# Inner values, outputs and divisions of a fused decoder layer set in other steps

## The chip, the cores and the metric

One core of one Trainium2 chip runs the whole kernel. The metric is device time in microseconds (us). Five engines take part: TensorE (PE in the profile; its weight loads are PEld), VectorE (DVE), ScalarE (ACT), GpSimd (POOL) and SyncE (SP), which here only issues transfers. Each engine works through its own list of instructions, and semaphores between them keep the data right.

## The reference

A decoder layer over `x` of 4 batches x 1024 tokens x 512 features, all float32, with a context of 4 x 1024 x 384. Cut to what matters:

```python
x = x + gated_attention(layernorm(x))             # 16 heads of 32; an aperture and an expression gate; a rotation of the result
q = layernorm(x) @ Wq + bq; k = ctx @ Wk + bk; v = ctx @ Wv + bv
x = x + softmax(q k^T / sqrt(32)) v @ Wo + bo     # cross attention, 16 heads
s = layernorm(x) @ Win + bin                      # 64 units
h = relu(s[..., None] * W1 + b1)                  # each with 16 inner values
g = sum_h(h * W2) + b2
x = x + g @ Wout + bout
```

The last four lines are 64 tiny networks of one input, 16 inner values and one output each, between two matrix products.

## The kernel before, in words

The work is cut into eight units: units 0 to 3 are the gated attention of batches 0 to 3, units 4 to 7 the cross attention of the same batches. A unit has two halves of 512 query tokens, and a half has 4 groups of 4 heads (`g`) with 8 key tiles of 128 (`kt`): 32 steps. The text names a step unit/half/step, so 5/1/4 is the fifth step of the second half of unit 5. The order of every engine's instructions is the order in which the program writes them; nothing reorders them.

A step (`step` in `attention`) does this, in this order:

- `issue_due(False)` runs what an earlier step left for this one (divisions).
- `scores`: TensorE computes two score tiles `s` of 128 x 1024 (L574), ScalarE makes the exponentials `e` of each (L579), VectorE adds them into `es` (L585, L587), two additions a step in units 4 to 6 and none at `kt` 0. There are two `s` tiles and six `e` tiles.
- `issue_due(True)` runs what was left to stand behind these additions.
- `late.pop(0)()` is the previous step's `times`: the exponentials times the values, into `av` (L601).

Eight steps end a group. ScalarE copies `av` out (L618), one step later the sums go through L631 and L632, and `sum_d` carries them through memory into another layout; two steps later `divide` takes reciprocals (L668), which travel through `rec_d` and come back spread over all partitions as `recb` (L671, L675); two steps after that `multiply` (L681) writes the divided values over the queries. `after(steps, f, behind)` puts such a part off: with `behind` it runs in `issue_due(True)`, without it in `issue_due(False)`.

Between the steps `run` lays other work, the filler. `beside(u, hf)` lists it: projections for the next unit, the output projection and layer norm of the half before (`post`: "wo", "load", "o", "ln"), and in units 5 to 7 the small networks of earlier halves. Every item has a load, about its matmuls in units of four; `run` spreads the sum of the loads evenly over the 32 steps. An item without a load goes into the step where the item before it ended. `pause(n)` makes n items that carry a load of 1 and do nothing. `weave(a, b)` sets the items of `a` evenly among those of `b`.

The small networks of a half go through these items: "s" makes `s` (L841), 17 items "h" make the inner values on ScalarE (`hid`, L858, two buffers) and add each, one item later, into `g` on VectorE (L862, L864). Two items "out" then multiply with `Wout`; each takes two tiles of the pool `f` (L875), adds them to the residual (L881) and sends it out (L883). The pool `f`, from `bank()`, has two PSUM tiles of 128 x 512 and serves every projection too (L87, evacuated at L280 to L284, L525, L770). `held` keeps a half whose inner values are not all made. The first few are made at the end of one `beside`, the rest at the start of the next by `end(items)`, which weaves them into `items` and sets the outputs behind. The last unit has no next projections and uses pauses.

Of the kernel before, what the change touches and what calls it, by code (L numbers as in the profile page):

```python
# [63 lines left out]
def moderate_path(tc: tile.TileContext, a: dict, out: bass.AP, flag: bass.AP):  # L64
    nc = tc.nc
    x = a["x"]
    with ExitStack() as st:
# [130 lines left out]
        def rotate(c):  # L198
            def f():
                pw = bank()  # L200
                columns(pw, rot[:, c, :], raw[0][:, c, :], start=True, stop=True)
                nc.vector.tensor_copy(raw[0][:, c, :], pw)
                if c == NC - 1:
                    nc.sync.dma_start(wout_d, raw[0])
            return [(1, f)]
# [130 lines left out]
        order = [(ph, b) for ph in range(2) for b in range(B)]  # L336
        n = len(order)
# [4 lines left out]
        def after(steps, f, behind=False):  # L342

            soon.append((tick[0] + steps, behind, f))
# [206 lines left out]
        def attention(u, hf):  # L551
# [8 lines left out]
            def apart(g):  # L560
                return 2 if u + 1 < len(order) else 3
# [90 lines left out]
            def divide(g, i, both, c):  # L652
                if shared:
                    both_ = p2.tile([P, sums, INNER], F32, tag="c2", name="both_")
                    nc.vector.tensor_tensor(both_, c[:, 0:sums, 0, :], c[:, 0:sums, 1, :], ALU.add)
                else:
                    both_ = c[:, 0:1, 0, :]
                if ph == 0:

                    den = p2.tile([P, INNER], F32, tag="den", name="den")  # L660
                    nc.vector.scalar_tensor_tensor(
                        den, both_[:, 0, :], 1e-8, me["iap", hf][:, g, :], ALU.mult, ALU.mult
                    )
                    nc.vector.tensor_tensor(den, den, both_[:, 1, :], ALU.add)
                else:
                    den = both_[:, 0, :]
                rec = p2.tile([P, INNER], F32, tag="rec", name="rec")
                nc.vector.reciprocal(rec, den)  # L668
                nc.vector.tensor_reduce(marks[:, i : i + 1], den, AX.X, ALU.add)
                nc.vector.tensor_reduce(marks[:, NS + i : NS + i + 1], rec, AX.X, ALU.add)  # L670
                nc.sync.dma_start(rec_d[i % 4].rearrange("j (q e) -> (j q) e", e=INNER), rec)  # L671

                all_ = p1.tile([P, HALF], F32, tag="recb", name="recb")
                for j in range(HG):
                    nc.sync.dma_start(  # L675
                        all_[j * DH : (j + 1) * DH, :], rec_d[i % 4][j : j + 1, :].to_broadcast([DH, HALF])
                    )
                after(apart(g), lambda: multiply(g, both, all_))

            def multiply(g, both, all_):  # L680
                nc.vector.tensor_tensor(me["q", hf][:, g, :], both[:, 0, :], all_, ALU.mult)  # L681
                me["divided", hf] = g
# [235 lines left out]
        def weave(light, items):  # L918

            first, second = sum(light, []), sum(items, [])  # L920
            out, done = [], 0
            for n, f in enumerate(first):
                upto = (2 * n + 1) * len(second) // (2 * len(first))
                out += second[done:upto] + [f]
                done = upto
            return [out + second[done:]]
# [14 lines left out]
        def pause(load):  # L941
            return [[(1, None)] * load]

        n = len(order)
        pres = [pre(u) for u in range(n)]

        def one(f):
            return [[(0, f)]]

        ending = []  # L950
        held = []

        def ahead(u, what):

            return one(lambda: pres[u]["load"](what))

        def some(half, k):

            h, half["h"] = half["h"][:k], half["h"][k:]
            return h  # L960

        def beside(u, hf):

            last = post(u, 0) if hf else post(u - 1, 1) if u else None
            end = lambda items: weave(held[0]["h"], items) + held.pop()["out"] if held else items
            if u + 1 == n:
                h, out = held[0]["h"], last["wo"] + last["load"]
                k = min(len(h), 6)
                if hf:
                    ending.append(post(u, 1))  # L970
                    out += ending[0]["wo"]
                out += weave(h[0:k], pause(12)) + weave(h[k:], last["o"]) + held.pop()["out"]
                out += (ending[0]["load"] if hf else []) + weave(last["ln"], pause(5)) + last["xT"]
                out += weave(last["b"], pause(8))
                out += weave(last["tr"], pause(3)) + last["s"] + weave(some(last, 8), pause(14))
                held.append(last)
                return out
            p = pres[u + 1]
            x, ln, xT, tr, k, q, v = (p[i] for i in ("x", "ln", "xT", "tr", "k", "q", "v"))
            next_ = pres[u + 2] if u + 2 < B else None  # L980
            if u + 1 < B:
                if hf == 0:
                    if last:
                        out = x[1] + last["wo"] + last["load"] + ahead(u + 1, "v") + k[0][0:1] + p["g"][0] + k[0][1:] + p["gt"][0]
                        out += weave(ln[1], last["o"]) + xT[1] + weave(last["ln"], v[0][0:2])
                    else:
                        out = one(fold_bv) + x[1] + k[0][0:1] + [rotate(c) for c in range(NC)]
                        out += ahead(u + 1, "v") + p["g"][0] + k[0][1:2] + [[(4, fold_bv)]] + weave(ln[1], k[0][2:])
                        out += p["gt"][0] + v[0][0:1] + xT[1] + v[0][1:2]
                    return out + tr[1] + v[0][2:3] + p["g"][1] + v[0][3:] + p["gt"][1]  # L990
                if not next_:
                    out = k[1] + ahead(u + 1, "q") + last["wo"] + last["load"] + v[1] + ahead(u + 2, "k") + last["o"]
                    return out + weave(last["ln"], q[0][0:2]) + q[0][2:] + pres[u + 2]["ctx"][0] + q[1]
                out = next_["x"][0] + k[1][0:2] + last["wo"] + last["load"] + weave(next_["ln"][0], k[1][2:] + v[1])
                out += ahead(u + 1, "q") + ahead(u + 2, "k") + last["o"]
                out += weave(last["ln"], q[0][0:2]) + q[0][2:] + next_["xT"][0] + q[1][0:3] + next_["tr"][0] + q[1][3:]
                if u == 1:
                    out = one(lambda: load_networks(0)) + out + one(lambda: load_networks(1)) + one(fold_bin)
                return out
            if hf == 0:  # L1000
                out = ahead(u + 1, "v") + last["wo"] + p["ctx"][1] + end(k[0] + v[0][0:1]) + last["load"] + v[0][1:2]
                out += last["o"] + weave(last["ln"], v[0][2:])
                if "s" in last:
                    out += last["xT"] + k[1][0:2] + weave(last["tr"], k[1][2:3]) + [k[1][3][0:2]] + last["s"]
                    held.append(last)
                    return out + xT[0] + weave(last["b"] + some(last, 5), [k[1][3][2:]] + v[1][0:2]) + tr[0]
                return out + k[1] + xT[0] + v[1][0:2] + tr[0]
            out = ahead(u + 1, "q") + last["wo"] + end(v[1][2:] + q[0][0:2]) + xT[1]
            out += (ahead(u + 2, "k") if u + 2 < n else []) + last["load"] + q[0][2:3] + last["o"] + tr[1]
            out += weave(last["ln"], q[0][3:] + q[1][0:1])  # L1010
            out += pres[u + 2]["ctx"][0] if u + 2 < n else []
            if "s" in last:
                out += last["xT"] + weave(last["b"], q[1][1:2]) + weave(last["tr"], q[1][2:3]) + [q[1][3][0:2]] + last["s"]
                held.append(last)
                return out + weave(some(last, 3), [q[1][3][2:]])
            return out + q[1][1:]

        p = pres[0]
# [16 lines left out]
        for u in range(n):  # L1035
            if u == 0:
                crossing.append(True)
            for hf in range(2):
                run(attention(u, hf), beside(u, hf))
# [8 lines left out]
        o, ln, b, tr, s = ([part for item in tail[k] for part in item] for k in ("o", "ln", "b", "tr", "s"))  # L1048
        h = [part for item in held[0]["h"] for part in item]
# [18 lines left out]
        h = sum(tail["h"], [])  # L1068
# [650 lines left out]
```

## Time and profile before

| | |
|---|---|
| median of 3 runs | 2214.34 us (2213.7 to 2214.6) |
| profiled execution | 2215.2 us, span 2213.4 us |
| matmuls busy (PE) | 2174.9 us, 98% |
| VectorE busy | 1564.7 us, 71% |
| ScalarE busy | 1237.5 us, 56% |
| exponentials L579 | 1024 of 1022 ns |
| additions L587 | 534 of 1227 ns |
| inner values L858, L864 | 128 of 604 ns, 120 of 481 ns |
| multiplications L681 | 63 of 689 ns, 17.0 us idle before them for `recb` |

A row of the timeline has a start and a length in us, the engine, the line, the operation, what it writes and reads, how often it stands there in a row, and in brackets the idle time ahead of it with what ended it. The chain of waits goes back from the last instruction, at each step to what released it. The windows view gives, for a stretch of time, its length, then the busy time of each engine and its instructions, TensorE's granted clock, the share of the DMA engines and the rate of transfers. A busy TensorE need not be at its full rate: the ends of matmuls are modelled.

### The profile page before, as it was taken

To read this page: it belongs to the slowest core of one execution; us is meant where nothing else is said; L and a number is where in the kernel's file an instruction comes from. 1 tells how busy PE (TensorE), PEld (TensorE's weight loads), DVE (VectorE), ACT (ScalarE), POOL (GpSimd) and SP (SyncE) were. 2 spreads that over 40 slices of the span, in tenths; PEclk is the share of its full clock that TensorE was granted. 3 is DMA by queue.
4 is the path that set the end of the run, shared out by engine and by line. 5 is a ranking of instruction groups with operands and counts; after the bars stand their busy time and mean duration, and the time that the engine had idled before them with its cause. 6 is when DMAs were issued, how large, how long until landed. Compare 5 with 4: busy or idle time off the path is not lost.

```text
span 2213.4 us, 52736 instructions
## 1 busy us (share of the span) xinstructions
PE 2174.9 (98%) x22598; PEld 548.2 (25%) x22598; DVE 1564.7 (71%) x2526; ACT 1237.5 (56%) x1489; POOL 84.2 (4%) x118
## 2 busy tenths in 40 slices
PE   8999999999999999999999999999999999999995
PEld 3322222222222222222222222222222222222222
DVE  4478675796757957577686666877777776856476
ACT  0155545555455554555656565666657565667673
POOL 1000000030300000000000000000000000000000
PEclk9999999999999999999999999999999999999998
DMA  4412123032330211211413032313223132303031
GB/s 144 136 51 71 47 98 108 22 88 66 100 108 23 85 66 55 79 39 54 106 36 108 26 87 64 111 50 69 76 79 83 64 90 66 88 12 114 24 88 40
DMA packets 153304, 161.70 MB, mean 73 GB/s; under 512 B 46202, under 2 KB 91898, under 8 KB 151908
## 3 DMA queue, kind: packets, MB, share of 16 engines
q1 hardware_dynamic: 149068, 156.14, 23.9%
q8 instruction: 179, 2.93, 0.5%
q0 software_dynamic: 2144, 0.98, 0.3%
q10 hardware_dynamic: 1848, 1.12, 0.2%
q14 instruction: 65, 0.53, 0.1%
HBM read 115.40 MB, written 42.74 MB: 71 GB/s over the span
## 4 chain that ended last, share of the span: by engine, by line
PE 93%; DVE 3%; ACT 2%; issue 1%; DMA 1%; SPq 0%; DVEq 0%; ACTq 0%
PE f L87 36%; PE s L574 25%; PE av L601 21%; PE sm L609 6%; PE sm L631 3%; ACT e L579 1%; DVE es L587 1%; DMA w<-in_attn_Wo 1%; PE f L875 1%; PE f L841 1%; DVE g L864 1%; ACT hid L858 0%; PE f L471 0%; PE s L87 0%; PE f L325 0%
## 5 line engine op out<-in xcount | busy, mean ns | idle before, releaser
L579 ACT ACTIVATE e<-s 128x1024 f32<-128x1024 f32 x1024 | 993.5, 1022 | 727.6 <-PE s L574 529.7
L587 DVE TENSOR_TENSOR es<-es,e 128x1024 f32<-128x1024 f32 x534 | 642.1, 1227 | 259.1 <-ACT e L579 257.7
L574 PE MATMUL s<-q,k 32*64 32x512 f32 x8192 | 608.8, 613 | 4.6 <-ACT e L579 3.3
L601 PE MATMUL av<-e,v 128*32 128x512 f32 x4096 | 551.1, 604 | 0.0
L87 PE MATMUL f<-xT,w 128*32 128x512 f32 x2816 | 334.1, 592 | 2.6 <-DVE res L881 2.4
L595 DVE SCALAR_TENSOR_TENSOR eg<-e,sw,eg 128x512 f32<-128x512 f32 x448 | 318.5, 747 | 2.3
L585 DVE TENSOR_TENSOR es<-e 128x1024 f32<-128x1024 f32 x89 | 106.7, 1222 | 204.1 <-ACT e L579 189.5
L574 PEld LDWEIGHTS s<-q,k 32*64 32x64 f32 x8192 | 133.5, 129 | 449.3 <-ACT e L579 243.6
L87 PE MATMUL f<-w,q 128*32 128x512 f32 x1984 | 240.1, 592 | 0.7 <-DVE q L720 0.7
L601 PEld LDWEIGHTS av<-e,v 128*32 128x32 f32 x4096 | 88.0, 108 | 404.6 <-issue 401.4
L87 PEld LDWEIGHTS f<-xT,w 128*32 128x32 f32 x2816 | 91.8, 110 | 213.8 <-issue 203.2
L609 PE MATMUL sm<-e,sw 128*2 128x512 f32 x1024 | 133.3, 592 | 0.0
L87 PE MATMUL f<-w,xT 128*32 128x512 f32 x896 | 106.0, 592 | 0.6 <-DVE q L284 0.6
L87 PEld LDWEIGHTS f<-w,q 128*32 128x32 f32 x1984 | 65.6, 110 | 149.5 <-issue 143.9
L87 PE MATMUL f<-w,ctxT 128*32 128x512 f32 x768 | 92.6, 592 | 0.0
L858 ACT ACTIVATE hid<-sT,units 128x256 f32<-128x256 f32 x128 | 76.6, 604 | 28.7 <-DVE g L864 21.0
L87 PE MATMUL f<-ctxT,w 128*32 128x512 f32 x768 | 92.3, 592 | 0.0
L778 POOL TENSOR_TENSOR r<-res,bo_bc 128x512 f32<-128x512 f32 x32 | 40.9, 1279 | 1040.1 <-DVE res L770 808.3
L864 DVE SCALAR_TENSOR_TENSOR g<-hid,units,g 128x256 f32<-128x256 f32 x120 | 57.7, 481 | 11.6 <-ACT hid L858 5.8
L631 PE MATMUL sm<-es,ones 128*1 128x512 f32 x348 | 65.8, 601 | 0.0
L681 DVE TENSOR_TENSOR q<-both,recb 128x512 f32<-128x512 f32 x63 | 43.6, 692 | 17.1 <-DMA recb<-rec_d 17.0
L770 DVE TENSOR_TENSOR res<-f,res 128x512 f32<-128x512 f32 x62 | 42.5, 686 | 17.5 <-PE f L87 17.2
(258 smaller groups left out, 1040.0 us busy)
## 6 DMA issues: line engine op xcount, KB each, us to landing
recb<-rec_d SPq DMA_DIRECT2D x252, 64.0 KB
xT<-rows_d SPq DMA_DIRECT2D x60, 256.0 KB
rows_d<-r SPq DMA_DIRECT2D x60, 256.0 KB
w<-in_xattn_Wo SPq DMA_DIRECT2D x9, 1024.0 KB
w<-wout_d SPq DMA_DIRECT2D x8, 1024.0 KB
res<-in_x SPq DMA_DIRECT2D x32, 256.0 KB
x1b_d<-r SPq DMA_DIRECT2D x32, 256.0 KB
res<-x1b_d SPq DMA_DIRECT2D x32, 256.0 KB
```

Source lines behind the costliest of these rows:

```text
L87: nc.tensor.matmul(to[r], lhsT=lhsT[:, j, :] if len(lhsT.shape) == 3 else lhsT[:, r], rhs=rhs, **flags)
L574: nc.tensor.matmul(s[m : m + 64, j, :], lhsT=k[r, g, kt * P + m : kt * P + m + 64], rhs=q[r, g, :], start=True, stop=True,)
L579: nc.scalar.activation(e, s, AF.Exp, scale=SCALE)
L585: nc.vector.tensor_tensor(me["es"][i], me["e", 0][i], es[i], ALU.add)
L587: nc.vector.tensor_tensor(me["es"][i], me["es"][i], es[i], ALU.add)
L595: nc.vector.scalar_tensor_tensor(eg, es[0][:, h, :], gate(kt), eg, ALU.mult, ALU.add)
L601: nc.tensor.matmul(av[r, :], lhsT=me["v"][:, kt, HG * g + h, :], rhs=es[h // 2][:, h % 2, :], start=(kt == 0), stop=(kt == NT - 1),)
L609: nc.tensor.matmul(sm[j * DH : j * DH + sums, :], lhsT=me["sw"][:, t, HG * g + 2 + h, :] if ph == 0 else ones, rhs=me["e", t][1][:, h, :], ...
L631: nc.tensor.matmul(sm[j * DH : j * DH + 1, :], lhsT=ones, rhs=e, start=True, stop=True)
L681: nc.vector.tensor_tensor(me["q", hf][:, g, :], both[:, 0, :], all_, ALU.mult)
L858: nc.scalar.activation(hid, res["s"], AF.Relu, bias=units[:, 1, h : h + 1], scale=units[:, 0, h : h + 1])
L864: nc.vector.scalar_tensor_tensor(res["g"], res["hid"], units[:, 2, h - 1 : h], res["g"], ALU.mult, ALU.add)
```

## The change

Four edits, in `divide` and `beside`.

```diff
@@ divide
-                after(apart(g), lambda: multiply(g, both, all_))
+                after(apart(g), lambda: multiply(g, both, all_), behind=u + 1 < len(order))
@@ beside
-            end = lambda items: weave(held[0]["h"], items) + held.pop()["out"] if held else items
+            end = lambda items: weave(held[0]["h"], items) + (lambda o: o[0:1] + pause(1) + o[1:] + pause(1))(held.pop()["out"]) if held else items
             if u + 1 == n:
...
-                out += weave(h[0:k], pause(12)) + weave(h[k:], last["o"]) + held.pop()["out"]
+                out += pause(2) + weave(h[0:k], pause(10)) + weave(h[k:], last["o"]) + held.pop()["out"]
...
             if hf == 0:
-                out = ahead(u + 1, "v") + last["wo"] + p["ctx"][1] + end(k[0] + v[0][0:1]) + last["load"] + v[0][1:2]
+                out = ahead(u + 1, "v") + last["wo"] + p["ctx"][1] + end(k[0] + v[0][0:2]) + last["load"]
                 out += last["o"] + weave(last["ln"], v[0][2:])
...
-            out = ahead(u + 1, "q") + last["wo"] + end(v[1][2:] + q[0][0:2]) + xT[1]
-            out += (ahead(u + 2, "k") if u + 2 < n else []) + last["load"] + q[0][2:3] + last["o"] + tr[1]
+            out = ahead(u + 1, "q") + last["wo"] + end(v[1][2:] + q[0][0:3]) + xT[1]
+            out += (ahead(u + 2, "k") if u + 2 < n else []) + last["load"] + last["o"] + tr[1]
```

First, `multiply` stands behind the two additions of its step and no longer ahead of them, in all units but the last. Second, `end` sets a pause behind each of the two outputs. Third, in the last unit the first two of twelve pauses come ahead of the inner values. Fourth, the inner values are woven into one more product: the second values' product in half 0, the third queries' product in half 1. That product stood behind the loads of the residual and now stands ahead of the outputs; the loads come behind the outputs, directly ahead of the output projection.

## The prediction

> I write 5/1/4 for step 4 of half 1 of unit 5; a step is one call of `step`: two score tiles, two exponentials, the matmuls of the previous step, then what `run` puts between.
>
> **What bounds the kernel now.** First the page's busy shares:
>
> ```profile
> PE 2174.9 (98%) x22598; PEld 548.2 (25%) x22598; DVE 1564.7 (71%) x2526; ACT 1237.5 (56%) x1489; POOL 84.2 (4%) x118
> ```
>
> TensorE is the bound, but 98% hides its losses. Its timeline gives a step's own work: 3.76 us with two eight-matmul pieces of filler (1600.06 to 1603.82), 2.90 with one (1607.57 to 1610.47), 2.04 with none, 0.85 more with the sums of L631. I subtracted that from each step's duration, scores to scores. From 225 us to 1430 us under 4 us are left. Units 5 and 6 lose 10.5 us each, and alike: the windows over 5/0/29 to 5/1/11 and over the same steps of unit 6 are
>
> ```profile
> core 0: us, PE busy (x) PEld busy (x) DVE busy (x) ACT busy (x) POOL busy (x), PEclk, DMA share, GB/s
> 1544.28:1607.57 63.29, 61.19 (x588) 14.62 (x584) 47.42 (x64) 43.20 (x59) 0.00 (x0) 1.00 0.39 90
> 1795.74:1859.04 63.30, 61.20 (x589) 14.62 (x585) 47.43 (x64) 43.20 (x59) 0.00 (x0) 1.00 0.36 85
> ```
>
> The 15 steps hold 55.67 us of TensorE work in 63.29 us: 7.6 us are lost, of which only 2.1 show as idle. Why, says the chain of waits from 1572 us:
>
> ```profile
> 1572.41 2.36 DVE es L587 x2
> 1574.77 0.41 DVE g L864
> ...
> 1575.27 0.60 ACT hid L858
> 1575.87 0.92 ACT e L579
> ...
> 1576.83 2.00 PE s L574 x16
> ```
>
> and ScalarE's timeline:
>
> ```profile
> 1573.17 0.61 ACT L858 ACTIVATE hid<-sT,units 128x256 f32<-128x256 f32 x1
> 1575.27 0.60 ACT L858 ACTIVATE hid<-sT,units 128x256 f32<-128x256 f32 x1 [1.49 <-DVE g L864]
> 1575.77 1.92 ACT L579 ACTIVATE e<-s 128x1024 f32<-128x1024 f32 x2
> 1577.58 0.59 ACT L858 ACTIVATE hid<-sT,units 128x256 f32<-128x256 f32 x1
> 1579.66 0.60 ACT L858 ACTIVATE hid<-sT,units 128x256 f32<-128x256 f32 x1 [1.49 <-DVE g L864]
> 1580.17 1.92 ACT L579 ACTIVATE e<-s 128x1024 f32<-128x1024 f32 x2
> ```
>
> A ring: `hid` has two buffers, so the second inner value of a step waits for a `g`, which stands behind the step's two additions, which wait for the exponentials; the next exponentials wait behind that inner value. With two inner values per step it turns in 1580.17 - 1575.77 = 4.40 us, not 3.76. The second loss is the outputs' banks:
>
> ```profile
> 1588.77 2.00 PE L875 MATMUL f<-wout,g 64*128 64x512 f32 x4
> 1590.69 1.11 PE L574 MATMUL s<-q,k 32*64 32x512 f32 x16
> 1591.74 1.06 PE L601 MATMUL av<-e,v 128*32 128x512 f32 x8
> 1592.99 2.00 PE L574 MATMUL s<-q,k 32*64 32x512 f32 x16 [0.18 <-ACT e L579]
> ...
> 1596.74 1.13 PE L875 MATMUL f<-wout,g 64*128 64x512 f32 x4
> 1599.06 1.07 PE L87 MATMUL f<-xT,w 128*32 128x512 f32 x8 [1.19 <-DVE res L881]
> ```
>
> L875 takes both banks of pool `f`; the first time it waits for `q` to be copied out (2.00 us for 1.13), the second time the product behind it waits 1.19.
>
> [...] the exponentials of 1575.77 had their scores by 1574.43 and stood behind the waiting inner value. [...]
>
> **Rules, from rows of before.** (1) Undisturbed exponentials start 1.15 us after the scores; the next scores' second tile needs both done. So a 2.90 us step costs the next 0.28 (scores 1.40 us instead of 1.11 at 1610.47), a 2.04 us step 1.14 (1590.69: 0.25 + 0.89). (2) Exponentials late by b cost b - 0.65 behind a 3.76 us step: those of 5/0/0 start at 1433.51, scores at 1431.19, b = 1.17, loss 0.51. Behind a 2.90 us step it is 0.86 more, behind 4.6 us 0.86 less. (3) One pair of inner values makes b = 4.40 - 3.76 = 0.64, hence alone nothing; a copy (L282, 0.6) behind it adds to b. (4) A step with one inner value brings b back to 0: at 1446.25 b was 1.3, at 1448.71 it was 0.
>
> **The change, part by part**, by the order of instructions in the changed program. Matmuls, inner values, copies and additions stay in number; they move.
>
> *Inner values over more products.* Half 1 of unit 5. Before: 16 inner values in 5/0/29 to 5/1/6, by step 1,3,1,2,1,2,2,2,1,1. After: in 5/0/30 to 5/1/7, by step 2,3,1,2,1,1,2,1,1,2. Before lost, step by step: 0.28 (5/0/29), 1.13 (three inner values in a row), then the ring 0.49+0.61+0.89+0.64 = 2.63. After: the 0.28 stays (5/0/27 is now the 2.90 step), three in a row stay, b about 1.7: 1.05; the pair in 5/1/1 lies in a 4.61 us step: 0; the pair in 5/1/4 with a `q` copy behind it: b = 1.24, 0.6; the pair in 5/1/7 has the 2.90 us step behind it: 0.64 - 0.65 + 0.86 = 0.85.
>
> *Room behind the outputs.* Before: 0.87 + 0.25 + 0.89 + 1.19 = 3.2. After, L875 stands in 5/1/9 and 5/1/11. The first still waits for the `q` copy: this follows L632 on ScalarE and starts when its product ends, 0.7 of copy against 0.47 of the first L875 matmul: 0.35. 5/1/10 holds no filler: 1.14. 5/1/11 is 2.97: 0.2. The next product needs the bank about when L881 frees it, 4.5 + 0.7 us after the scores of 5/1/11 against 3.16 + 2.04: 0.1.
>
> Other short steps: before 5/1/12, 20, 28: 0.84. After 5/1/12, 24: 0.56. Sum for half 1: before 0.28+1.13+2.63+3.2+0.84 = 8.1, after 0.28+1.05+0.6+0.85+0.35+1.14+0.3+0.56 = 5.1; gain 3.0.
>
> Half 0 of unit 5: from 5/0/0 the inner values stood 3,2,2,1,2,2,1,0, now 2,2,1,2,2,1,2,1. Before: 0.49 (5/0/1), 0.63 (5/0/4), 1.08 and 0.13 at the outputs (5/0/7, 8): 2.3. After: 0.51 stays (nothing changes ahead of it); pairs in 5/0/3 and 5/0/4 follow each other, with a `k` copy: b = 1.3, 0.67; the pair in 5/0/6 has a 4.62 us step behind it: 0; short steps 8, 10, 11: 0.28+0.2+0.28. Together 1.9; gain 0.4.
>
> Unit 6 has the same order: 2 x 3.4 = 6.8.
>
> *The last unit's pauses.* Nothing: an inner value has no load, so `run` puts it into the same step; no instruction of unit 7 moves for it. Units 0 to 4 have no `held`.
>
> *Multiplications behind the additions.* 56 of 63 (unit 7's seven stay), 0.69 us each, same work. They waited 17.0 us for `recb`, in 11 places; TensorE lost nothing there (steps 3.76 around the longest, 5.31 us, ended 1617.51), so its end gains nothing: 0. Below: -1 if it helps DVE reach a `g`. Above: in 5/0/5 and 5/1/5 the multiplication now stands ahead of a `g` instead of in idle time; if that inner value were awaited, 4 x 0.6 = 2.4. I take 0: both inner values start behind exponentials that end later. It reads no bank; it stands ahead of a bank's reader (L525, L770) in 5 steps, 0.6 us; by the steps' times that bank is next written 3 us or more later. `both` and `recb` are next written at least 3 steps later.
>
> *Loads on SP.* In half 1 the four `res` loads now stand closer to their use: behind the second outputs, `xT` and `Wk`. At 231 GB/s (window 1600.06 to 1607.57) the 2.1 MB up to the first `res` take 9.1 us; by my count it lands 2 us after DVE is ready for L770. Queued behind L770 are the additions of 5/1/15, whose six `e` buffers leave three steps, and a bank needed 5 us later. So 0; late by more than 5 us each us would cost one.
>
> **Sum.** Own execution 2215.2 us (span 2213.4, 1.8 around it): 2208.4. It lies 0.9 above the median 2214.34, so 2207.5 in the median.
>
> **Rivals.** *Half of it* (0.20): the pairs that I cost at 0 (5/0/3, 5/0/6, 5/1/1) lose 0.9 each like before's ring: three of them take 2 x 2.7 = 5.4 us of the gain, two 3.6; 2211 to 2213. For: three in a row remain. Against: rule 4. *More* (0.12): the pairs in 5/0/4, 5/1/4 and 5/1/7 cost nothing, since DVE no longer runs late: 2.1 a unit more, 2203. *The ring does not break* (0.08, slower): if one-value steps don't recover, the ten steps 5/1/0 to 5/1/9 run at 4.4 plus a 0.6 copy, 5.0 instead of 3.76: 12 us a unit, of which my sum has 3; 2 x 9 more, about 2225. It passes 2214.3 + 4.4 when these steps lose 0.6 us each beyond my sum. Against it: 1448.71. *No effect* because the order did not change: excluded, it does.
>
> **How the numbers follow.** Mine, 2205 to 2209.9: 0.60. 0.2% is 4.4 us, about what a measurement of this kernel can tell from none. Faster: 0.60 + 0.12; same 0.20; slower 0.08. The range 2203 to 2212.5 leaves out the ring and the ends.
>
> **What would show it.** Right: in 5/1/4 to 5/1/6 steps of 3.76 with at most one 0.6 loss; TensorE's 1.19 wait for L881 gone; a 3.2 us step at 5/1/10; idle before L681 near 0. Wrong: inner values waiting for `g` in successive steps; L770 waiting for a load with TensorE idle behind it; losses in units 0 to 4.

## The result, and the profile after

The changed kernel takes 2210.85 us (median of 16 runs, 2209.36 to 2212.84); the kernel before, on the same chip, 2214.96 us (16 runs). The ratio is 0.9981, 95% interval 0.9975 to 0.9988: 4.1 us, or 0.19%, faster, where 6.8 us were predicted. The profiled execution has a span of 2210.6 us, 2.8 less than before. Single executions of one kernel differ by some 2 us either way (the kernel before: 2213.7 to 2217.13), so beside each time I use a steadier measure, worked out of TensorE's timeline as in the prediction: a step's duration, scores to scores, less its own work. I call it the step's loss.

The page, busy shares and the group of multiplications:

```profile
PE 2174.1 (98%) x22598; PEld 547.7 (25%) x22598; DVE 1562.2 (71%) x2526; ACT 1238.5 (56%) x1489; POOL 82.0 (4%) x118
...
L681 DVE TENSOR_TENSOR q<-both,recb 128x512 f32<-128x512 f32 x63 | 43.3, 687 | 7.5 <-DMA recb<-rec_d 7.5
```

The first line hides the change entirely, as it hid the losses before. The second has 7.5 us of waiting for `recb` where the prediction wanted "near 0" (17.0 before); what is left says more than its size, see below.

The windows over 5/0/29 to 5/1/11 and over the same steps of unit 6:

```profile
core 0: us, PE busy (x) PEld busy (x) DVE busy (x) ACT busy (x) POOL busy (x), PEclk, DMA share, GB/s
1544.91:1604.36 59.45, 59.20 (x580) 14.11 (x576) 44.10 (x60) 43.65 (x58) 0.00 (x0) 1.00 0.25 62
1793.40:1852.86 59.46, 59.21 (x581) 14.11 (x577) 44.11 (x60) 43.66 (x58) 0.00 (x0) 1.00 0.24 62
```

These 15 steps took 63.3 us before and take 59.5 now, though 0.9 us of that is work that left the window (580 matmuls for 588). The ring turns once and stops. ScalarE's timeline at the pair in 5/1/4:

```profile
1574.22 1.94 ACT L579 ACTIVATE e<-s 128x1024 f32<-128x1024 f32 x2 [1.33 <-PE s L574]
1576.05 0.60 ACT L858 ACTIVATE hid<-sT,units 128x256 f32<-128x256 f32 x1
1578.13 0.60 ACT L858 ACTIVATE hid<-sT,units 128x256 f32<-128x256 f32 x1 [1.48 <-DVE g L864]
1578.64 0.67 ACT L282 ACTIVATE q<-f,bqk 128x512 f32<-128x512 f32 x1
1579.21 1.93 ACT L579 ACTIVATE e<-s 128x1024 f32<-128x1024 f32 x2
1581.02 0.60 ACT L858 ACTIVATE hid<-sT,units 128x256 f32<-128x256 f32 x1
1581.73 1.94 ACT L579 ACTIVATE e<-s 128x1024 f32<-128x1024 f32 x2
```

The pair and the copy L282 make the exponentials 4.99 us apart (1574.22, 1579.21); behind the one inner value of the next step they are 2.52 apart (1581.73) and on time again. And the outputs, on TensorE's timeline:

```profile
1595.18 1.04 PE L87 MATMUL f<-xT,w 128*32 128x512 f32 x8
1596.15 2.00 PE L875 MATMUL f<-wout,g 64*128 64x512 f32 x4
1598.09 1.11 PE L574 MATMUL s<-q,k 32*64 32x512 f32 x16
...
1600.38 2.00 PE L574 MATMUL s<-q,k 32*64 32x512 f32 x16 [0.18 <-ACT e L579]
1602.31 1.06 PE L601 MATMUL av<-e,v 128*32 128x512 f32 x8
1603.30 1.13 PE L875 MATMUL f<-wout,g 64*128 64x512 f32 x4
1604.36 1.11 PE L574 MATMUL s<-q,k 32*64 32x512 f32 x16
```

The product that waited 1.19 us for L881 is gone from here. The first output still takes 2.00 us for 1.13, and the empty step shows as 2.00 us of scores behind it.

So these steps gained what was forecast for them, about 3.0 us in each of the two units. What was given back elsewhere shows in the chain of waits ahead of unit 7 (unit 7 starts at 1929.01):

```profile
1908.83 0.49 SPq L312
...
1909.36 5.61 DMA sum_d<-both
1914.97 0.02 issue
1914.99 1.54 DMA cs<-sum_d
...
1916.55 0.25 DVE rec L668
...
1930.74 0.34 DVE g L862
...
1931.16 0.13 ACT hid L858
...
1932.33 0.92 ACT e L579
...
1933.30 2.89 PE s L574 x14
```

Read it downwards: the load of `xn` on SP, a write and a read through memory that were issued behind it, a reciprocal, 14 us of VectorE without a break, the first `g`, the inner value that waits for it, the exponentials, the scores. Before, no transfer stands in this chain. The losses by part, in us:

| | before | after | gain |
|---|---|---|---|
| 5/0 and 5/1 | 2.80 + 7.91 | 2.48 + 5.13 | 3.1 |
| 6/0 and 6/1 | 2.81 + 7.91 | 2.61 + 5.69 | 2.4 |
| 7/0 | 13.66 | 15.60 | -1.9 |

Of these, 5/0/0 and 5/0/1 went from 0.48 to 1.01, 6/0/0 and 6/0/1 from 0.48 to 1.13, 6/1/30 from 0 to 0.56, 7/0/0 to 7/0/2 from 3.88 to 5.81. The gains add up to 3.6 us, the span is 2.8 shorter: unit 5 starts 0.4 us later than before, and 0.4 is lost behind 7/0.

### The profile page after: what moved, and what is told of

Read it like the earlier page. It is cut to its first block, busy times and chain, and to the rows that moved or that the text cites. A ratio compares the mean times of both kernels' runs of the same rounds, so it can differ in the third digit from the quotient of the medians.

```text
span 2210.6 us, 52746 instructions
## 1 busy us (share of the span) xinstructions
PE 2174.1 (98%) x22598; PEld 547.7 (25%) x22598; DVE 1562.2 (71%) x2526; ACT 1238.5 (56%) x1489; POOL 82.0 (4%) x118
## 4 chain that ended last, share of the span: by engine, by line
PE 92%; DVE 3%; issue 2%; DMA 2%; ACT 2%; SPq 0%; DVEq 0%; ACTq 0%
PE f L87 35%; PE s L574 24%; PE av L601 21%; PE sm L609 6%; PE sm L631 3%; DVE es L587 1%; ACT e L579 1%; PE f L875 1%; DMA xn<-rows_d 1%; DVE g L864 1%; PE f L841 1%; DMA rows_d<-r 0%; PE f L325 0%; PE f L471 0%; PE f L1025 0%
## 5 line engine op out<-in xcount | busy, mean ns | idle before, releaser
L574 PE MATMUL s<-q,k 32*64 32x512 f32 x8192 | 608.7, 614 | 4.5 <-ACT e L579 2.9
L601 PE MATMUL av<-e,v 128*32 128x512 f32 x4096 | 551.1, 604 | 0.0
L87 PE MATMUL f<-xT,w 128*32 128x512 f32 x2816 | 333.7, 592 | 0.6 <-PE f L87 0.6
L574 PEld LDWEIGHTS s<-q,k 32*64 32x64 f32 x8192 | 133.1, 130 | 449.4 <-ACT e L579 243.3
L87 PE MATMUL f<-w,q 128*32 128x512 f32 x1984 | 240.5, 592 | 0.7 <-DVE q L720 0.7
L601 PEld LDWEIGHTS av<-e,v 128*32 128x32 f32 x4096 | 88.1, 108 | 404.6 <-issue 401.4
L87 PEld LDWEIGHTS f<-xT,w 128*32 128x32 f32 x2816 | 92.1, 110 | 211.3 <-issue 204.4
L87 PE MATMUL f<-w,xT 128*32 128x512 f32 x896 | 106.0, 592 | 0.6 <-DVE q L284 0.6
L87 PEld LDWEIGHTS f<-w,q 128*32 128x32 f32 x1984 | 65.5, 110 | 150.0 <-issue 142.3
L87 PE MATMUL f<-w,ctxT 128*32 128x512 f32 x768 | 92.6, 592 | 0.0
L87 PE MATMUL f<-ctxT,w 128*32 128x512 f32 x768 | 92.3, 592 | 0.0
L631 PE MATMUL sm<-es,ones 128*1 128x512 f32 x348 | 65.8, 601 | 0.0
L770 DVE TENSOR_TENSOR res<-f,res 128x512 f32<-128x512 f32 x62 | 42.5, 686 | 17.9 <-PE f L87 8.9
L681 DVE TENSOR_TENSOR q<-both,recb 128x512 f32<-128x512 f32 x63 | 43.3, 687 | 7.5 <-DMA recb<-rec_d 7.5
```

What stands on the lines that cost most here:

```text
L87: nc.tensor.matmul(to[r], lhsT=lhsT[:, j, :] if len(lhsT.shape) == 3 else lhsT[:, r], rhs=rhs, **flags)
L574: nc.tensor.matmul(s[m : m + 64, j, :], lhsT=k[r, g, kt * P + m : kt * P + m + 64], rhs=q[r, g, :], start=True, stop=True,)
L601: nc.tensor.matmul(av[r, :], lhsT=me["v"][:, kt, HG * g + h, :], rhs=es[h // 2][:, h % 2, :], start=(kt == 0), stop=(kt == NT - 1),)
L631: nc.tensor.matmul(sm[j * DH : j * DH + 1, :], lhsT=ones, rhs=e, start=True, stop=True)
```

## The experiments

My first theory (A) was that the multiplications, now between the additions and the layer norms L303, make the transposes' transfer late. Its rival (B): the two pauses set everything behind them half a step later. The table has all kernels, with the times of before on the same chip (not all kernels ran on one chip, so the ratios are what compares them); "3/1, 4/1" to "7/0" are losses in the profiled execution:

| kernel | median us (before) | ratio, 95% | 3/1, 4/1 | unit 5 | unit 6 | 7/0 |
|---|---|---|---|---|---|---|
| before | | | 2.10 | 10.71 | 10.72 | 13.66 |
| changed | 2210.85 (2214.96) | 0.9981, 0.9975 to 0.9988 | 2.10 | 7.61 | 8.30 | 15.60 |
| no multiplication edit | 2213.87 (2214.8) | 0.9996, 0.9988 to 1.0005 | 4.61 | 7.17 | 8.00 | 15.58 |
| multiplication edit only | 2215.65 (2214.8) | 1.0006, 0.9998 to 1.0015 | 2.10 | 11.32 | 11.32 | 11.99 |
| pauses only | 2217.86 (2214.8) | 1.0013, 1.0006 to 1.0019 | 2.11 | 11.22 | 10.14 | 16.07 |
| one more product only | 2213.38 (2214.8) | 0.9994, 0.9986 to 1.0003 | 3.97 | 7.84 | 10.43 | 11.99 |
| loads of units 3, 4 back | 2211.98 (2214.92) | 0.9989, 0.9980 to 0.9997 | 2.10 | 7.15 | 8.00 | 14.43 |
| norms a product closer | 2212.59 (2214.92) | 0.9990, 0.9982 to 0.9999 | 2.10 | 9.74 | 9.82 | 11.99 |
| before, norms later | 2231.26 (2214.92) | 1.0075, 1.0061 to 1.0089 | 4.92 | 20.44 | 12.36 | 14.54 |
| changed, again | 2211.09 (2214.92) | 0.9981, 0.9974 to 0.9988 | 2.10 | 7.09 | 8.14 | 16.13 |
| norms half a step early | 2208.73 (2215.53) | 0.9970, 0.9959 to 0.9981 | 2.09 | 7.52 | 7.55 | 14.16 |
| and transposes later | 2211.50 (2215.53) | 0.9982, 0.9974 to 0.9990 | 2.10 | 7.53 | 8.36 | 14.55 |
| norms early, `xT` earlier | 2207.21 (2214.47) | 0.9966, 0.9954 to 0.9978 | 3.11 | 7.09 | 7.08 | 13.63 |
| norms half a step early, again | 2208.35 (2214.47) | 0.9972, 0.9960 to 0.9984 | 2.09 | 7.52 | 7.56 | 13.64 |

### The multiplications taken out, and alone

```diff
-                after(apart(g), lambda: multiply(g, both, all_), behind=u + 1 < len(order))
+                after(apart(g), lambda: multiply(g, both, all_))
```

The reverse of this is the only edit of the second run.

> The changed kernel with the multiplications L681 back ahead of the additions; the other three edits stay. Theory A (the multiplications, now directly ahead of the layer norms L303, make the transposes' transfer late, VectorE waits for it, and the exponentials of 6/0/0, 6/0/1, 7/0/0, 7/0/1 come late): the missing gain comes back, about 3.5 us below the changed kernel, so about 2207.4, ratio to before 0.9965 to 0.997, and the losses of 6/0/0 and 6/0/1 fall from 1.1 to about 0.5 us, those of 7/0/0 and 7/0/1 from 5.7 to about 3.9. Theory B (the pauses and the later output projection make the transfer late, the multiplications do nothing): as the changed kernel, ratio 0.998, losses at 6/0/0 and 7/0/0 unchanged.

> The kernel before with only the multiplications L681 moved behind the additions. Theory A: slower by 1.5 to 3.5 us, ratio 1.0007 to 1.0016, with the added losses at 5/0/0 and 5/0/1, 6/0/0 and 6/0/1, 7/0/0 and 7/0/1. Theory B: no difference, ratio 0.9997 to 1.0003, losses at those steps as before. The prediction on record priced it at 0, bounds -1 to +2.4 us.

Theory A falls. Without the edit 6/0/0 and 6/0/1 still lose 1.03 us and 7/0/0 and 7/0/1 still 5.70; with it alone they lose what they lose before, or less (2.21 in place of 3.88, a matter of TensorE's clock, see the last section). But the ratio without it is 0.9996: the edit is worth 0.0015, about 3 us, in the changed kernel (the two intervals just touch), and nothing or a little less than nothing alone. The profile without it shows where, in units that I had called untouched: 3/1/16 loses 1.44 us and 4/1/17 1.05. VectorE, then TensorE, there:

```profile
1125.59 0.69 DVE L681 TENSOR_TENSOR q<-both,recb 128x512 f32<-128x512 f32 x1 [5.50 <-DMA recb<-rec_d]
1126.20 1.22 DVE L587 TENSOR_TENSOR es<-es,e 128x1024 f32<-128x1024 f32 x1
```

```profile
1128.47 1.09 PE L574 MATMUL s<-q,k 32*64 32x512 f32 x8
1129.93 1.09 PE L574 MATMUL s<-q,k 32*64 32x512 f32 x8 [0.38 <-ACT e L579]
```

The multiplication, ahead of the additions, holds VectorE up for 5.50 us; the six `e` buffers don't cover that, and the scores are torn in two. SP's timeline in the same execution says why `recb` is late:

```profile
1111.34 1.91 SPq L745 DMA_DIRECT2D res<-in_x  x4
1113.34 0.38 SPq L671 DMA_DIRECT2D rec_d<-rec  x1
1120.68 2.95 SPq L675 DMA_DIRECT2D recb<-rec_d  x4
```

L675 reads what L671 writes, and that small write (128 x 16 numbers) is issued behind four loads of `res`: 7.3 us from one issue to the other. In the changed kernel, which has the same order there, SP's wait at this place is shown as one for `rec_d`, 6.7 us, while the share of the DMA engines is 0.93 to 1.16 from 1112 to 1119 and 0.13 in the next us, before L675 goes out at 1120.71. The fourth edit had moved those loads, in units 3 and 4 too.

The edit alone costs 0.6 us each in 5/0/7 and 6/0/7 (1.09 to 1.69). ScalarE in 5/0/6, before and then with the edit:

```profile
1457.20 0.60 ACT L858 ACTIVATE hid<-sT,units 128x256 f32<-128x256 f32 x1 [0.67 <-DVE g L864]
```

```profile
1458.43 0.60 ACT L858 ACTIVATE hid<-sT,units 128x256 f32<-128x256 f32 x1 [1.27 <-DVE g L864]
```

The inner value starts 1.49 us behind the scores of 5/0/6 (1455.71) before, 2.10 us with the edit (1456.33): the awaited `g` stands behind the multiplication. In the changed kernel the pairs lie in other steps and this cost is not there.

### The loads of units 3 and 4 put back

```diff
-                out = ahead(u + 1, "v") + last["wo"] + p["ctx"][1] + end(k[0] + v[0][0:2]) + last["load"]
+                out = ahead(u + 1, "v") + last["wo"] + p["ctx"][1] + (end(k[0] + v[0][0:2]) + last["load"] if held else k[0] + v[0][0:1] + last["load"] + v[0][1:2])
...
+            more, out = (q[0][2:3], []) if held else ([], q[0][2:3])
+            out = ahead(u + 1, "q") + last["wo"] + end(v[1][2:] + q[0][0:2] + more) + xT[1] + (ahead(u + 2, "k") if u + 2 < n else []) + last["load"] + out
```

Without the multiplication edit, as above; against that run only SP's list differs.

> The changed kernel without its multiplication edit, with the residual's loads of units 3 and 4 put back ahead of the last product woven in; only SP's list differs from the run without the multiplication edit, whose profile lost 1.4 us at 3/1/16 and 1.1 us at 4/1/17 behind multiplications that waited 5.5 and 4.2 us for recb. Theory C (those loads, issued directly ahead of rec_d and recb, make recb late, and the additions stand behind the multiplication): both losses go, the two waits fall under 2 us, and it is 2.5 us faster than that run, ratio to before 0.9985. Theory D (recb's landing varies by itself from one execution to the next, the loads have nothing to do with it): the waits of 4 to 5 us stay in 3/1 and 4/1 or move, ratio 0.9996.

Theory C holds. SP in the same place:

```profile
1110.72 0.33 SPq L671 DMA_DIRECT2D rec_d<-rec  x1
1112.14 1.74 SPq L675 DMA_DIRECT2D recb<-rec_d  x4
```

1.4 us instead of 7.3, L681 no longer waits there or in 4/1, and both losses are 0 again. The losses there fall by the 2.5 us that were expected; the median is 1.9 us lower, but on another chip, and the intervals of the two ratios overlap, so it is the profile that decides here. In the changed kernel `recb` is just as late (L671 at 1112.86, L675 at 1120.71); there the multiplication behind the additions covers it, and the waits of 2.4 us at 3/1/15 and 1.7 at 4/1/15 in its profile cost nothing. So one part of the change repairs what another broke. That the loads ahead of the write make `recb` late is what the 7.3 and 1.4 us show; in which order transfers are served and end, no run here tests. The kernel before has the same pattern in another place: in 5/1, L671 is issued at 1606.41 right behind four loads of `res`, and L675 only at 1613.97, with 6.2 us of waiting for `rec_d` on SP. There it costs nothing (L681 waits 5.31 us, and the steps from 1614.51 and 1618.27 take 3.76 and 3.75), and in the changed kernel it is gone (1602.91 and 1604.35).

### The pauses alone, the product alone

```diff
-            end = lambda items: weave(held[0]["h"], items) + held.pop()["out"] if held else items
+            end = lambda items: weave(held[0]["h"], items) + (lambda o: o[0:1] + pause(1) + o[1:] + pause(1))(held.pop()["out"]) if held else items
```

```diff
-... end(k[0] + v[0][0:1]) + last["load"] + v[0][1:2]
+... end(k[0] + v[0][0:2]) + last["load"]
...
-... end(v[1][2:] + q[0][0:2]) + xT[1]
-            out += (...) + last["load"] + q[0][2:3] + last["o"] + tr[1]
+... end(v[1][2:] + q[0][0:3]) + xT[1]
+            out += (...) + last["load"] + last["o"] + tr[1]
```

> The kernel before with only a pause behind each of the two outputs in units 5 and 6. By the prediction's sums the two waits for a bank at the outputs (2.0 us per second half with the short steps between) go: about 1.5 us a unit faster, so 3 us, ratio about 0.9986, with the ring of inner values in 5/1/2 to 5/1/6 as before. Theory A: nothing lost at 6/0/0 and 7/0/0 beyond the kernel before. Theory B: extra losses there of about 0.6 and 1.8 us, and the ratio is 0.9995 or more.

> The kernel before with only the inner values woven into one more product and the residual's loads behind the outputs. By the prediction's sums the ring of 5/1/2 to 5/1/6 loses about 1.5 us instead of 2.6, and the outputs still wait for their banks: about 1.5 us a unit faster, so 3 us, ratio about 0.9986. Theory A: no extra loss at 6/0/0 and 7/0/0. Theory B: part of the extra loss of 0.6 and 1.8 us there shows here, because the output projection stands one product later in the second halves.

Both sizes were missed, and theory B is half confirmed. The pauses alone are slower than before. They do take the losses at 5/1/7 to 5/1/9 from 3.64 to 1.37 us, but 6/0/0 and 6/0/1 lose 1.05 and 7/0/0 and 7/0/1 5.69, as in the changed kernel; and `recb` comes 8.6 us late at 5/1/15, again with L671 right behind four loads of `res` (8.4 us from L671 to L675), which costs 2.5 at 5/1/16 and 5/1/17. The product alone shows none of the extra loss at 6/0/0 and 7/0/0; it gains 2.9 us in unit 5, but only 0.3 in unit 6, where the product behind the outputs waits 2.11 us for L881 and TensorE is at about half its rate after it (from 1854.59 eight matmuls of L87 in 1.93 us, 16 of L574 in 2.01 and eight of L601 in 1.94, where 1.04, 1.11 and 1.06 are usual); and it pays 1.9 in 3/1 and 4/1. The third edit, two pauses ahead of the last unit's inner values, was not run alone; the traces of before and of the changed kernel list unit 7's own instructions in the same order on every engine.

### The norms earlier, and later

```diff
-            out += weave(last["ln"], q[0][3:] + q[1][0:1])
+            out += weave(last["ln"], q[0][3:]) + q[1][0:1] if "s" in last else weave(last["ln"], q[0][3:] + q[1][0:1])
```

on the changed kernel, and on the kernel before

```diff
-            out += weave(last["ln"], q[0][3:] + q[1][0:1])
+            out += [q[0][3][0:2]] + weave(last["ln"], [q[0][3][2:]] + q[1][0:1] + [q[1][1][0:2]]) if "s" in last else weave(last["ln"], q[0][3:] + q[1][0:1])
...
-... weave(last["b"], q[1][1:2])
+... weave(last["b"], [q[1][1][2:]])
```

> The changed kernel with the four norms L303 of the second halves (4/1, 5/1, 6/1) set one product closer together; TensorE's and ScalarE's lists are the same, VectorE's and SP's differ in the place of the norms alone. Theory B (the norms come late behind the pauses, the transposes L318 wait for xn, the first g is late, ScalarE and then TensorE wait, and the idle TensorE gets half its clock): VectorE's wait ahead of L318 falls from 4 us to under 2, the first g L862 goes back from 1.4 and 1.6 us behind the scores to 0.73, the losses of 6/0/0 and 6/0/1 fall from 1.1 to 0.5, those of 7/0/0 and 7/0/1 from 5.7 to 2.2 or 3.9, 6/1/30 to 0: 2.9 to 4.9 us below the changed kernel, ratio to before 0.9960 to 0.9968. If the first g is late for another reason: as the changed kernel, 0.998.

> The kernel before with the norms L303 of the second halves half a step later and nothing else: TensorE's and ScalarE's lists are unchanged. Theory B: L318 waits for xn as in the changed kernel, losses at 6/0/0 and 6/0/1 rise from 0.5 to about 1.1, at 7/0/0 and 7/0/1 from 2.2 to 3.9 up to 5.7: slower than before by 2.5 to 5 us, ratio 1.001 to 1.0023. If the norms don't matter: 1.000.

First the changed kernel itself at the end of unit 6, VectorE's timeline:

```profile
1915.12 0.71 DVE L318 STREAM_TRANSPOSE xn<-xn 128x512 f32<-128x512 f32 x1 [4.04 <-DMA xn<-rows_d]
...
1926.11 4.63 DVE L587 TENSOR_TENSOR es<-es,e 128x1024 f32<-128x1024 f32 x4
1930.65 0.41 DVE L862 TENSOR_SCALAR g<-hid,units,fb 128x256 f32<-128x256 f32 x1
```

It waits 4.04 us for `xn`, is still working off additions without a break at 7/0/0, and reaches the first `g` 1.64 us behind the scores of 7/0/0 (1929.01). Before, the same wait is 0.45 us:

```profile
1917.76 0.71 DVE L318 STREAM_TRANSPOSE xn<-xn 128x512 f32<-128x512 f32 x1 [0.45 <-DMA xn<-rows_d]
...
1932.57 2.36 DVE L587 TENSOR_TENSOR es<-es,e 128x1024 f32<-128x1024 f32 x2 [1.41 <-ACT e L579]
1934.85 0.41 DVE L862 TENSOR_SCALAR g<-hid,units,fb 128x256 f32<-128x256 f32 x1
```

There VectorE is idle again ahead of the last pair, and `g` comes 0.73 us behind the scores (1934.12). Counted back from unit 7's first scores, the load of `xn` goes out 24.0 us ahead of them before, and 24.0 and 24.1 with the product alone and the multiplications alone; it is 21.6 in the changed kernel and 21.8 with the pauses alone. So the pauses move it, but not by half a step throughout: the last norm is only 0.4 us later and VectorE asks for `xn` 1.1 us sooner. The other 2 us lie between the last norm and the load, which waits until the norm's rows are written (SP waits 3.6 us for `rows_d` there, 1.7 before); why that takes longer there stays open.

With the norms closer together every start and loss that theory B gave came true: the wait ahead of L318 is 0.7 us in 5/1 and nothing in 6/1, L862 at 0.73 in 6/0/0 and 7/0/0, losses 0.48 at 6/0/0 and 6/0/1, 0 at 6/1/30, 2.20 at 7/0/0 and 7/0/1. The time did not follow (2212.59 us), because 5/1/25 and 6/1/25 now lose 2.9 us each:

```profile
1650.27 0.55 DVE L303 TENSOR_SCALAR r<-res,fmv,yi 128x512 f32<-128x512 f32 x1 [1.70 <-DMA rows_d<-r]
1650.73 2.36 DVE L587 TENSOR_TENSOR es<-es,e 128x1024 f32<-128x1024 f32 x2
```

The third norm of a row waits for its buffer to be written out, and the additions behind it, which the sums L631 need, are late. With the norms later on the kernel before, the sign was right, but the size was far off, 16 us for at most 5, and so were the places: 5/0/0 and 5/0/1 lose 5.3 us, 5/1/30 4.9 and 6/1/30 1.7, while 6/0/0 and 6/0/1 lose 0.48 as before. The load of `xn` fell behind the next sums' transfers on SP, L318 waited 6.75 us at the end of 5/1, and TensorE itself for the transposed tile:

```profile
1688.79 3.22 PE L841 MATMUL f<-xn,win 128*32 128x256 f32 x28 [2.83 <-DVE xn L318]
```

So this round trip through memory has little to spare before, and nothing after.

### The changed kernel again

> The changed kernel once more, for the loss of 0.5 us that its profile alone shows at 5/0/0 and 5/0/1, and for the half clock at 7/0/1. Ratio 0.998. If 5/0/0 is an accident of that execution, its loss is as before, 0.48 over both steps; if it belongs to the change, 1.0 again. TensorE idles over 2 us at 7/0/0 and its clock is half for 6.8 us again, since both follow from the late g.

The time is the same. The 1.0 us at 5/0/0 and 5/0/1 was an accident of one execution: here it is 0.48, as before, with L318 waiting 2.4 us instead of 3.3 at the end of 4/1. The loss of 7/0, where TensorE stood idle and then ran at half clock in the first execution, came again: 16.13 us for 15.60.

### A better place for the norms

```diff
-            out += weave(last["ln"], q[0][3:] + q[1][0:1])
+            out += weave(last["ln"], q[0][3:] + [q[1][0][0:2]]) + [q[1][0][2:]] if "s" in last else weave(last["ln"], q[0][3:] + q[1][0:1])
```

and, in the second run, with it

```diff
-... weave(last["b"], q[1][1:2]) + weave(last["tr"], q[1][2:3]) + ...
+... [q[1][1][0:1]] + weave(last["b"], [q[1][1][1:] + q[1][2][0:1]]) + weave(last["tr"], [q[1][2][1:]]) + ...
```

> The changed kernel with the last norm L303 of the second halves one pair of additions (half a step) earlier, and never three norms in a row; TensorE's and ScalarE's lists are the same. The run with the norms one product closer lost 2.9 us at 5/1/25 and 6/1/25, where the third norm of a row waited 1.7 us for its buffer to be written out and the additions stood behind it. Theory B with that: the waits of L318 for xn fall from 4 us to about 2, the first g is at 0.73 behind the scores in 6/0/0 and 7/0/0, nothing is lost at 5/1/25 beyond 0.3: losses 0.5 at 6/0/0 and 6/0/1, 2.2 to 3.9 at 7/0/0 and 7/0/1. 2.5 to 4.5 us below the changed kernel, ratio to before 0.9961 to 0.9970, and faster than both. If norms at this distance still hold the additions up: 1 to 3 us lost at 5/1/25 and 6/1/25, ratio 0.9975 to 0.999.

> As the run before it, and the transposes L318 of xn one eighth of a product's four parts, that is one piece of filler, later, so that they are asked for when xn is there. Theory B: VectorE's wait ahead of L318 falls under 1.5 us; losses at 6/0/0, 6/0/1, 7/0/0 and 7/0/1 as in that run; ratio to before 0.9961 to 0.9970 too. If it overshoots, TensorE waits for the transposed tile (L841 at 6/1/30, more than 0.3 us lost there).

The first beats the kernel before: 2208.73 us. Its ratio is also below that of the changed kernel, 0.9970 for 0.9981, but the intervals overlap; in the profiles it loses about 2 us less than the changed kernel's repeat. The waits for `xn` are 3.3 and 3.0 us, not the expected 2; `g` comes at 0.73 in 6/0/0 and at 1.27 in 7/0/0, so 6/0/0 and 6/0/1 lose 0.48, 7/0/0 and 7/0/1 4.38, and 5/1/25 0.64. In the second the transposes were asked for one of a product's four parts later, and L318 waited for nothing. That did not help; the gain went back in the median (the two intervals overlap), 1.2 us of it in the profile. VectorE waits one instruction further on, for the transfer issued behind `xn`:

```profile
1916.12 0.25 DVE L668 RECIPROCAL rec<-cs 128x16 f32<-128x16 f32 x1 [3.97 <-DMA cs<-sum_d]
...
1930.82 0.41 DVE L862 TENSOR_SCALAR g<-hid,units,fb 128x256 f32<-128x256 f32 x1
```

So the named wait is not the cause. The sums that L668 waits for were copied out by 1904.67 (end of L632), but SP issues their transfer only at 1908.99, since the load of `xn` stands ahead of it in SP's list and goes out at 1907.03. Before, the same step takes 1.1 us in place of 4.3. The load of `xn` is late, and whoever comes first behind it waits.

The last run keeps the first edit and takes 2.6 us of VectorE's work out of the way of the norms:

```diff
-            out += (ahead(u + 2, "k") if u + 2 < n else []) + last["load"] + last["o"] + tr[1]
+            out += (ahead(u + 2, "k") if u + 2 < n else []) + last["load"] + (last["o"][0:2] + tr[1] + last["o"][2:] if "s" in last else last["o"] + tr[1])
```

> The changed kernel with the last norm half a step earlier (as two runs before) and the four transposes L318 of the next unit's xT, 4 x 0.65 us on VectorE directly ahead of the norms, moved two output projection tiles earlier; only VectorE's list differs. Theory B: VectorE has 2.6 us less to do ahead of the norms, so the last norm ends up to 1.7 us sooner (5/1/24 and 3.6 instead of 5/1/25 and 1.6), the first g of 7/0/0 goes from 1.27 to 0.73 behind the scores, and the 0.65 us at 5/1/25 and 6/1/25 go: losses at 7/0/0 and 7/0/1 2.2 or 3.9 instead of 4.4, together 1.8 to 3.5 us below the run with the norms alone, ratio to before 0.9954 to 0.9962. If the transposes hold up the additions at their new place: as that run or slower, 0.997 or more.

> The run with the norms half a step early once more, beside the one above on the same chip: ratio to before 0.9970 again, 0.9960 to 0.9980. Loss at 7/0/0 and 7/0/1 2.2 to 4.4 us, by whether TensorE's clock falls to half there after it has idled.

The last norm starts 2.24 us into 5/1/24 (1.59 into 5/1/25 with the first edit alone), `xn` is there when asked for in 6/1, and VectorE is idle again ahead of the last pair:

```profile
1910.80 0.70 DVE L318 STREAM_TRANSPOSE xn<-xn 128x512 f32<-128x512 f32 x1
...
1926.71 2.36 DVE L587 TENSOR_TENSOR es<-es,e 128x1024 f32<-128x1024 f32 x2 [1.41 <-ACT e L579]
1928.99 0.41 DVE L862 TENSOR_SCALAR g<-hid,units,fb 128x256 f32<-128x256 f32 x1
```

2207.21 us, 7.3 below before, is the lowest median of all, though the ratio expected was 0.9954 to 0.9962. Unit 6 loses 7.08 now, as much as unit 5. In 4/1, where the transposes moved too, 4/1/17 loses 1.0 us that it did not lose before. Beside it the run with the norms alone was 0.9972 again. Nothing here tells the two apart: their intervals overlap, and the table's losses come to 30.9 and 30.8 us, since the 0.9 us gained in units 5 and 6 are lost again in 4/1.

## Why the prediction was partly right

**Direction, and the two units: right.** Half 1 of unit 5, with the steps 28 to 31 of half 0 that the sum takes in, was summed to 5.1 us and lost 5.35. Inside, one term was too small (the first L875 lost 0.87 where 0.35 were summed), the pair of 5/1/7 cost nothing in its own step and 0.86 behind the short step 5/1/8, where the rule had it, and 5/1/10 with 5/1/11 lost 1.27 of 1.34. The rest of half 0 lost 1.74 of 1.9 in the undisturbed execution (0.52 more in the first, at 5/0/0). In the undisturbed execution, units 5 and 6 without 6/0/0, 6/0/1 and 6/1/30 gained 7.3 us, against the 6.8 of the sum.

**The step that failed: "Room behind the outputs" priced inside its own half.** What its two pauses do to the work behind them stood in no term of the sum, and so counted as nothing. ("The last unit's pauses. Nothing" is right for what it speaks of: none of unit 7's own instructions changed its place.) In the second halves of units 5 and 6 the pauses make the load of `xn` late, and I followed only the residual's loads and the banks. That load ends a round trip on which the first `g` of the next half depends. In the repeated execution it gave back 0.79 us at 6/0/0 and 6/0/1, 0.26 at 6/1/30 and 2.47 in 7/0: 3.5 of 7.3. (The 2.47 are counted from the one profile of before, in which 7/0 also lost 1.7 us to half clock; the last section has more.) The pauses alone show these losses, the product alone and the multiplications alone don't, and earlier norms take them away. How far each was moved by the pauses and how far by VectorE's backlog is not separated.

**"Loads on SP. So 0": wrong, and hidden.** I asked when L770 gets its residual. The transfer that suffers is the small one behind the loads, `rec_d`, and in units 3 and 4, which I dismissed with "have no held", a sentence true of the pauses alone. It costs 2.5 us in the profile where the multiplication stands ahead of the additions. That another edit covered it in the changed kernel was luck: I had foreseen neither.

**"Multiplications behind the additions: 0": wrong both ways.** Alone it costs 1.2 us in the profile, by the case I bounded with 2.4. In the changed kernel it is worth 2.5 us in the profile and about 3 in the medians, since it covers the late `recb`. I had read "TensorE lost nothing there" from the waits of before, in an order of loads that the change did not keep.

**The rivals.** The measured 2210.85 us lie just above the band of my own sum, 2205 to 2209.9. *Half of it* comes near in size (2211 to 2213, a gain of 1.3 to 3.3 us where 4.1 were measured), but its reason is not there: no pair that I had at 0 lost anything. *More* and *the ring does not break* are excluded by 5/1/6 (0.58) and by the steps behind each single inner value. Of the 7.5 us left ahead of L681, where I had wanted 0, 4.2 in 3/1 and 4/1 were the sign of the moved loads. The other 3.3 lie in unit 7, whose own multiplications did not move and waited 3.2 us before: there 0 could not have come.

## What to carry to other kernels

A pause put in for one bank moves all that stands behind it: follow the moved work to its end, through memory and into the next stage, and ask who waits there first. Before large loads are moved on a queue, look for the small write issued behind them (7.3 us from L671 to L675 here, 1.4 without the loads ahead) and for its reader, which holds up what stands behind it in its engine's list (VectorE for 5.50 us here); put behind other work, that reader is an insurance which shows no gain by itself. And when a wait is taken away, look one instruction further before you call it the cause.

## What was not expected of the hardware

TensorE's idle time was paid for twice. The windows of the changed kernel around 7/0/0, with the granted clock as the third number from the end:

```profile
1931.00:1933.00 2.00, 0.12 (x4) 0.00 (x0) 1.03 (x3) 1.84 (x3) 0.00 (x0) 1.00 0.02 4
1934.00:1935.00 1.00, 1.00 (x12) 0.31 (x8) 0.00 (x0) 1.00 (x3) 0.00 (x0) 0.50 0.00 0
1938.00:1939.00 1.00, 1.00 (x10) 0.00 (x0) 0.89 (x1) 0.90 (x2) 0.00 (x0) 0.50 0.00 0
1940.00:1941.00 1.00, 1.00 (x20) 0.16 (x8) 0.00 (x0) 0.06 (x1) 0.00 (x0) 1.00 0.00 0
```

When matmuls start again after 2.17 us without one (1931.13 to 1933.30), the clock is half, 0.50 from 1934 to 1939. With 0.57 granted in 1933 to 1934 and 0.52 in 1939 to 1940, the half clock lasts from 1933.14 to 1939.96, 6.8 us. In the kernel before, 1.27 us of idle time at the same place was followed by 3.4 us of it (1939.44 to 1942.84, worked out alike), which by this estimate cost half of that, 1.7 us:

```profile
1940.00:1941.00 1.00, 1.00 (x8) 0.19 (x4) 0.00 (x0) 1.00 (x2) 0.00 (x0) 0.50 0.00 0
```

With only one more product the same 1.27 us was followed by none (1.00 granted from 1938 to 1941), and none shows with only the multiplications moved: behind 1.27 us of idle time the eight matmuls of L631 took 1.04 us, where they took 1.89 in the changed kernel. Both lost 11.99 us in 7/0, and so did the kernel with the norms a product closer. Over all fourteen profiled executions the losses of 7/0 fall into three groups: 11.99 us three times, 13.63 to 14.55 seven times, 15.58 to 16.13 four times. Of the kernels whose clock is given here, those without half clock are in the first group, the kernel before, with 3.4 us of it, in the second and the changed kernel, with 6.8 us, in the third. The length of the idle time does not decide it alone: the same 1.27 us came with none and with 3.4 us. By the estimate above 3.4 us of half clock are 1.7 us lost and 6.8 at most 3.4, where the kernel before lies 1.67 us above 11.99 and the changed kernel, which stands idle 0.90 us longer, 3.61: this is most of why 7/0 differs from one execution to the next. What sets the lengths of 3.4 and 6.8 us is not shown. Whether the kernel before falls to half clock there mostly or seldom stays open: there is one profile of it.
